# A graph network's first layer: another PSUM bank for the second pick of a step, a ranking's count taken half a step later, two buffers for a sorter's rows

## The chip, the cores and the metric

The kernel runs on one core of a Trainium2 chip. The metric is the device time of one execution in microseconds: the median of three runs of the kernel before is 4270.91 us (4266.38 to 4275.15).

## What is computed

Three layers of graph attention over 6250 nodes and 206250 edges (100000 pairs both ways, and a loop at each node), sorted by target node, with 64 features each. The reference, cut to what matters:

```python
for i in range(3):
    q = x @ Wq + bq; k = x @ Wk + bk; v = x @ Wv + bv; e = edge_attr @ We
    kj = k[src] + e
    alpha = sum(q[dst] * kj, -1) / sqrt(64)
    p = exp(alpha - segment_max(alpha, dst)[dst])
    w = p / segment_sum(p, dst)[dst]
    x = segment_sum((v[src] + e) * w[:, None], dst) + x @ Ws + bs
    x = relu(x)
    if i < 2: x = layer_norm(x, gamma[i], beta[i])
y = layernorm(x_in + log_softmax(x))
```

## The kernel before

Edges are cut into chunks of 512, and four chunks make a unit; a layer is a line of some 100 units. A unit is an online piece of attention: its edges' source features are gathered or picked, turned (transposed) so that PE can make scores from them, exponentiated, turned back and summed with weights into the nodes.

**The order** is written out by hand: the five engines take their instructions in the order of the code, with waits only where tiles are shared. The loop of layer 0 stands near the end of `main_path`; a step u of it works on several units at once:

- `weights` (the probabilities of unit u-2, turned by PE into bank `p`, copied by ACT);
- `turn(0)`, a piece of the sorter, `sums` (bank `g`, copied out by ACT at L1725), another piece of the sorter;
- `scores` of unit u-1 into bank `s` (L1673, L1678 on PE; DVE takes the row maximum, L1685 and L1687);
- `naturals` of unit u+1 and the **first pick** for unit u+2 (`picker.bank`, L1374 on PE into bank `g`, then ACT's copy into `kept`, L1383), then DVE's four hot masks for the next pick (`aim`, L1331);
- `turn(1)` (L1650 on PE, two copies on ACT at L1653), then `exps` of unit u-1 (L1692 on ACT: it reads bank `s`);
- the third piece of the sorter, then the **second pick** (L1374 and L1383 again, also in bank `g`), and the fourth piece.

Between these, gates on ACT (L635) release the gathers of POOL, and nodes are finished and projected (`finish`, `project`; both use bank `g` too, at L1532 and L1446).

**PSUM** has eight banks here: two each for the tags `a` and `x`, one each for `s`, `p`, `g` and `m`. Who writes a bank waits until the one who wrote it before has been read.

**A pick** takes source features out of node blocks with a matmul against 0/1 masks ("hot"), in place of gathering them: 24 matmuls of three bf16 parts, four blocks and two halves. In layer 0 two picks are due in each step.

**The sorter** runs in layer 0 alone, in four pieces a step (`move`). It puts a unit's edge features into the places that the picks ask for: `products` (L1064, bank `x`), `codes` (L1078, bank `m`), masks by DVE (`row`, L1053), then `drain`. `across` turns the placed features back into natural rows (PE, L1102, bank `m` or `a`), ACT copies them into a tile `eN` (L1104), and a DMA that ACT issues stores them (L1107). `index` (L1115 to L1120 on PE) makes indices and keys, which DVE and ACT copy out (L1123, L1129, L1134).

**A ranking** (L932 to L941) gives seats to edges by their kind, 23 rounds for each of four groups of chunks; the sorter takes a half round at two or three places of a step (`next(orders)`). The first half of a round is four matmuls with the masks `kinds` (L928), an activation on ACT that adds the count of the round before (`served`, L932), the next masks (L920) and the next count, taken by DVE from the last column (L935); the second half is two more DVE instructions (L939, L940). The tile `eN` is also used as room at a ranking's start and in the kernel's setup.

Of the kernel before, what the change touches and what calls it, by code (L numbers as in the profile page):

```python
# [9 lines left out]
F32 = mybir.dt.float32  # L10
# [9 lines left out]
P = 128  # L20
D = 64
L = 3
T = 4
# [419 lines left out]
def main_path(  # L443
# [89 lines left out]
    sorts = first_layer.enter_context(tc.tile_pool(name="sorts", bufs=2))  # L533

    def ps(tag):
        return psum.tile([P, 512], F32, tag=tag, name=f"ps_{tag}", bufs={"a": 2, "x": 2}.get(tag, 1))
# [356 lines left out]
    def ranking(i):  # L893

        those, n = ranks[i]
        seat = sorts.tile([P, CH], FP16, name="seat")[:n]
        half = sorts.tile([P, T, P], FP16, name="half", bufs=1)
        bins = sorts.tile([P, CH], FP16, name="bins", bufs=1)[:n]
        served = sorts.tile([P, WINDOWS + 2], F32, name="served", bufs=1)
        room = sorts.tile([P, 2 * T * D], F32, name="eN", bufs=1).bitcast(I32)  # L900
        runs = []
        for r, c0 in those:
            if runs and runs[-1][1] + runs[-1][2] == c0:
                runs[-1][2] += GC
            else:
                runs.append([r, c0, GC])
        for r, c0, m in runs:
            v = room[:, : m * T]
            nc.vector.tensor_scalar(v, src_b[:, c0 * T : (c0 + m) * T], P.bit_length(), None, ALU.logical_shift_right)
            nc.vector.tensor_copy(half[:, :, r : r + m], v.rearrange("p (c t) -> p t c", t=T))  # L910
        pc = ps("a")[:n]
        for t in range(T):
            nc.tensor.matmul(pc[:, t * P : (t + 1) * P], half[:, t, :n], same, start=True, stop=True)
        nc.scalar.copy(bins, pc)
        nc.vector.tensor_scalar(seat, bins, float(WINDOWS), 1000.0, ALU.is_gt, ALU.mult)
        nc.vector.memset(served[:, 0:1], -1.0)

        def kinds_of(h):
            kinds = sorts.tile([P, T, P], FP16, name="kinds", bufs=2)[:, :, :n]
            nc.vector.tensor_scalar(kinds, half[:, :, :n], float(h), None, ALU.is_equal)  # L920
            return kinds

        kinds = kinds_of(0)
        yield
        for h in range(WINDOWS + 1):
            pc = ps("a")[:n]
            for t in range(T):
                nc.tensor.matmul(  # L928
                    pc[:, t * P :], kinds[:, t], past[:, : CH - t * P], start=(t == 0), stop=(t == T - 1)
                )  # L930
            order = sorts.tile([P, CH], FP16, name="order", bufs=1)[:n]
            nc.scalar.activation(order, pc, AF.Identity, bias=served[:n, h : h + 1])  # L932
            if h < WINDOWS:
                kinds = kinds_of(h + 1)
            nc.vector.tensor_scalar(  # L935
                served[:n, h + 1 : h + 2], order[:, CH - 1 :], float(SL * min(h + 1, WINDOWS) - 1), None, ALU.min
            )
            yield
            nc.vector.scalar_tensor_tensor(order, bins, float(h), order, ALU.is_equal, ALU.mult)  # L939
            nc.vector.tensor_tensor(seat, seat, order, ALU.add)  # L940
            yield  # L941
        left = sorts.tile([P, CH], FP16, name="order", bufs=1)[:n]
        nc.vector.tensor_scalar(bins, bins, float(WINDOWS - 1), float(SL), ALU.min, ALU.mult)
        nc.vector.scalar_tensor_tensor(left, seat, -float(SL), bins, ALU.add, ALU.is_ge)
        nc.vector.tensor_tensor_scan(bins, left, left, float(SLOTS - 1), ALU.add, ALU.max)
        yield
        nc.vector.copy_predicated(seat, left.bitcast(mybir.dt.uint16), bins)
        spans = small.tile([P, WINDOWS + 1 + T], F32, name="spare")[:n]
        nc.vector.tensor_tensor(spans[:, : WINDOWS + 1], served[:n, 1:], least[:n], ALU.subtract)
        nc.vector.tensor_tensor(spans[:, WINDOWS + 1 :], most[:n], bins[:, P - 1 :: P], ALU.subtract)  # L950
        nc.vector.tensor_reduce(lacks[:n, i : i + 1], spans, AX.X, ALU.min)
        ranked[i] = seat
        yield
# [57 lines left out]
    class Move:  # L1011
# [86 lines left out]
        def across(self, i):  # L1098

            pn = ps("ma"[i])  # L1100
            for t in range(T):
                nc.tensor.transpose(pn[:, t * P : (t + 1) * P], self.eT[i][:, t * P : (t + 1) * P], ident)  # L1102
            eN = sorts.tile([P, 2 * T * D], F32, name="eN", bufs=1)
            nc.scalar.copy(  # L1104
                eN.rearrange("p (j t d) -> p t j d", j=2, d=D), pn.rearrange("p (t j d) -> p t j d", j=2, d=D)
            )
            nc.scalar.dma_start(eaP[self.k, :, 2 * i * T * D : 2 * (i + 1) * T * D], eN)  # L1107
# [35 lines left out]
    def sorter():  # L1143
# [11 lines left out]
        for i, _ in enumerate(first_ranks):  # L1155
            if i % 2:
                yield
        begun = 1
        orders = ranking(begun)
        for _ in mark(marked.pop(0)[0]):  # L1160
            pass
# [589 lines left out]
    release(0, 2 * LB)  # L1751
    locate(NK - 1, NC - (NK - 1) * P)
    first_ranks = ranking(0)
    active.append(begin(*groups[1]))
    active.append(late())
# [90 lines left out]
    for layer in range(L):  # L1846
# [5 lines left out]
        def drip(u, n=1):  # L1852
            points[0] += n
            lead = 2 * LB if not layer else min(2 * LB, LB + u)
            most = LB * (T - 1) if not layer else LB + 1
            release(layer, u * LB + min(points[0], most) * LB / most + lead, nc.scalar.copy)
            if not layer:
                next(first_ranks, None)

        if not layer:  # L1860
            picker = Picker(layer)
        for u in range(NU - 3):
# [52 lines left out]
            close_up(3) if close else step()  # L1915
            move(paces[2])
            while picker.due(u + 2):
                picker.bank(u + 2, "g")
            drip(u)
            picker.load()  # L1920
            move(paces[3])
# [14 lines left out]
        if more:  # L1936
            picker = Picker(layer + 1)
# [6 lines left out]
        u = NU - 3  # L1944
# [80 lines left out]
def kernel(tc: tile.TileContext, *args):  # L2025
    nc = tc.nc
    with tc.tile_pool(name="flag", bufs=1) as pool:
        irregular = pool.tile([1, 1], I32, name="irregular")
        with tc.manual_schedule(engines={ENG.PE, ENG.DVE, ENG.Activation, ENG.SP, ENG.Pool}):
            main_path(tc, *args, irregular)  # L2030
        flag = nc.values_load(irregular[0:1, 0:1], min_val=0, max_val=1, skip_runtime_bounds_check_because="a comparison")
        with tc.If(flag > 0):
            general_path(tc, *args)
# [34 lines left out]
```

## Time and profile before

| | |
|---|---|
| Median of three runs | 4270.91 us (4266.38 to 4275.15) |
| The profiled execution's own time | 4275.86 us |
| Its span, first to last instruction | 4274.1 us |
| Its mean granted clock of TensorE | 0.948 |
| L1374, picks into bank `x` (layers 1 and 2), PE | 836.7 us, 13248 matmuls |
| L1374, picks into bank `g` (layer 0), PE | 302.3 us, 4560 matmuls |
| L1692, exponentials, ACT | 204.2 us, 297 |
| L1104, natural rows' copies in layer 0, ACT | 57.3 and 56.7 us, 98 each |

How to read it: PE is TensorE's matmuls, PEld its weight loads, which overlap them; DVE, ACT, POOL and SP are the vector, scalar, GpSimd and sync engines. A group's row gives the line, engine, operation, tiles written and read, shapes and count, then its busy time in all, the mean of one in ns, and the idle time of the engine just ahead of its instructions with what ended most of it. In a row of waits stand the total, the times and the longest in us. In a timeline the first column is the start and the second the length in us; in brackets stand the idle time of the engine ahead of it and what ended that. A row of a stretch gives its bounds and length, busy time and count for PE, PEld, DVE, ACT and POOL, then the granted share of the clock, the DMA share and GB/s. Ends of matmuls are modelled.

### The profile page before, as it was taken

The page shows a single profiled execution, that of the slowest core. Times are in us where ns is not written, and L with a number is a line of the kernel's source. Part 1 is how long each engine was busy: PE and PEld are TensorE (multiplying, and loading weights), DVE is VectorE, ACT ScalarE, POOL GpSimd, SP SyncE. Part 2 cuts the span into 40 slices and gives each one's busy share as a digit, 9 for nine tenths or more (in the row PEclk, how much of TensorE's full clock was granted, in tenths as well). Part 3 has the DMA queues.
Part 4 walks back from the last instruction along what each step waited for, and adds up shares of the span by engine and source line. Part 5 has one row for each costly group of instructions (what it writes and reads, how often), then busy time and mean ns, then how long its engine had stood idle before and what let it go on. Part 6 is the DMA issues. An engine that isn't in the chain of part 4 may idle for free.

```text
span 4274.1 us, 125157 instructions
## 1 busy us (share of the span) xinstructions
PE 3681.7 (86%) x44542; PEld 2464.7 (58%) x44542; DVE 2891.1 (68%) x9241; ACT 2394.9 (56%) x7113; POOL 2067.3 (48%) x1910
## 2 busy tenths in 40 slices
PE   4679998889999999987889999998778998888885
PEld 2345555555555655654666666666456666666663
DVE  5566888787788777774566666666456666666664
ACT  2334555555555555543566666666536676666664
POOL 4454554555455665552444444444415444444442
PEclk9789999999999999997999999999879999999997
DMA  5447787787777888874677777777647777777773
GB/s 119 101 131 188 201 213 203 192 211 200 206 198 211 226 212 209 218 196 131 146 183 189 192 185 186 188 193 182 152 96 191 177 181 184 187 186 179 176 187 83
DMA packets 828647, 768.02 MB, mean 180 GB/s; under 512 B 393233, under 2 KB 628903, under 8 KB 828014
## 3 DMA queue, kind: packets, MB, share of 16 engines
q1 hardware_dynamic: 673282, 571.05, 54.2%
q10 hardware_dynamic: 93932, 126.48, 8.4%
q0 software_dynamic: 60800, 62.38, 7.8%
q8 instruction: 356, 5.83, 0.6%
q14 instruction: 277, 2.27, 0.2%
HBM read 599.30 MB, written 160.27 MB: 178 GB/s over the span
## 4 chain that ended last, share of the span: by engine, by line


## 5 line engine op out<-in xcount | busy, mean ns | idle before, releaser
L601 POOL DMA_INDIRECT feat<-in_x,gate x860 | 1050.6, 1222 | 884.4 <-ACT gate L635 686.4
L1331 DVE TENSOR_SCALAR hot<-key,rank 128x512 bf16<-128x512 f16 (+3 forms) x3024 | 908.2, 350 | 372.5 <-PE ps_x L1374 167.5
L601 POOL DMA_INDIRECT feat<-x,gate x816 | 796.8, 976 | 745.3 <-ACT gate L635 479.1
L1374 PEld LDWEIGHTS <-halves 128*64 128x64 bf16 x18144 | 963.4, 113 | 285.7 <-issue 206.1
L1374 PE MATMUL ps_x<-hot,halves 128*64 128x256 bf16 (+1 forms) x13248 | 836.7, 276 | 41.6 <-issue 31.2
L1717 PE MATMUL ps_g<-feat,probT 128*32 128x128 f32 x9672 | 436.5, 283 | 92.4 <-issue 61.6
L1064 PE MATMUL ps_x<-hit,rest 128*64 128x512 bf16 (+3 forms) x3200 | 459.1, 359 | 6.0 <-issue 5.1
L1409 ACT COPY featT<-kept 64x512 f32<-64x512 f32 x584 | 361.5, 619 | 144.3 <-PE ps_g L1374 42.6
L1053 DVE TENSOR_SCALAR hit<-ruler,pos 128x512 bf16<-128x512 f16 (+3 forms) x1600 | 422.9, 334 | 1.7 <-PE ps_m L1078 1.4
L1717 PEld LDWEIGHTS ps_g<-feat,probT 128*32 128x32 f32 x9672 | 286.5, 112 | 221.5 <-issue 175.6
L1685 DVE TENSOR_REDUCE most<-ps_s 128x1 f32<-128x512 f32 x297 | 204.1, 687 | 300.6 <-PE ps_s L1678 111.9
L601 POOL DMA_INDIRECT few<-x,gate x198 | 193.6, 978 | 379.4 <-ACT gate L635 113.0
L1374 PE MATMUL ps_g<-hot,halves 128*64 128x256 bf16 (+2 forms) x4560 | 302.3, 281 | 74.1 <-ACT kept L1383 28.5
L1653 ACT COPY featT<-ps_a 64x512 f32<-64x512 f32 x584 | 338.6, 580 | 15.6 <-PE ps_a L1650 4.1
L1678 PE MATMUL ps_s<-featT,q 128*32 128x512 f32 x2376 | 333.7, 621 | 2.9 <-ACT featT L1653 1.3
L1064 PE MATMUL ps_x<-hit,raw 128*64 128x512 bf16 (+3 forms) x1600 | 311.0, 367 | 4.5 <-issue 4.1
L1383 ACT COPY kept<-ps_x 128x256 f32<-128x256 f32 (+2 forms) x502 | 185.1, 370 | 210.8 <-remote 128.6
L635 ACT COPY gate<-src_b 128x1 int32<-128x1 int32 x1762 | 289.9, 191 | 8.7 <-ACT keys L1136 1.4
L1692 ACT ACTIVATE prob<-ps_s,part 128x512 f32<-128x512 f32 x297 | 204.2, 688 | 161.0 <-issue 48.7
L1704 PE MATMUL ps_p<-ident,prob 128*128 128x128 f32 (+1 forms) x1224 | 199.1, 286 | 91.9 <-ACT prob L1692 89.8
L1064 PEld LDWEIGHTS <-rest 128*64 128x64 bf16 x3200 | 203.8, 113 | 116.6 <-issue 30.0
L1725 ACT COPY part<-ps_g 128x128 f32<-128x128 f32 (+1 forms) x309 | 82.2, 266 | 273.0 <-PE ps_g L1717 43.8
(261 smaller groups left out, 5162.4 us busy)
## 6 DMA issues: line engine op xcount, KB each, us to landing
feat<-eaP SPq DMA_DIRECT2D x292, 512.0 KB
featT<-eaS SPq DMA_DIRECT2D x292, 512.0 KB
key<-keyS SPq DMA_DIRECT2D x712, 128.0 KB
raw<-in_ea SPq DMA_DIRECT2D x200, 256.0 KB
eaS<-eT ACTq DMA_DIRECT2D x200, 256.0 KB
eaP<-eN ACTq DMA_DIRECT2D x200, 256.0 KB
to<-toS SPq DMA_DIRECT2D x292, 128.0 KB
part<-part SPq DMA_DIRECT2D x600, 32.5 KB
```

Source lines behind the costliest of these rows:

```text
L601: nc.gpsimd.indirect_dma_start(out=spares[layer, k] if c is None else loaded[layer, k][:, c, t, 0], out_offset=None, in_=xts[layer][:, :], ...
L635: copy(gate, index[:, i : i + 1])
L1053: nc.vector.tensor_scalar(hit, ruler[:, : REACH[t]], self.pos[:, at : at + 1], None, ALU.is_equal)
L1064: nc.tensor.matmul(self.px[i][j * D : (j + 1) * D, : REACH[t]], self.part(i, part)[:, (j * T + t) * D : (j * T + t + 1) * D], self.hits[t, ...
L1331: nc.vector.tensor_scalar(hot[:, a:b].rearrange("p k w e -> p (k w e)"), self.keys[job][:, a * 2 * SL : b * 2 * SL], rank[:, h : h + 1], None,
L1374: nc.tensor.matmul(px[w * D : (w + 1) * D, a:b], third(halves[block >= EARLY][:, at : at + 1], part)[:, 0], made[h][:, a:b, w], start=(h = ...
L1409: nc.scalar.copy(featT[:D, :, w * P : (w + 1) * P], kept[0][w * D : (w + 1) * D, at : at + LB])
L1653: nc.scalar.copy(self.featT[:D, :, at : at + P], pt[h * D : (h + 1) * D])
L1678: nc.tensor.matmul(self.p_s[rows], self.q[:, j * STRIDE : j * STRIDE + W], self.featT[:, j, :], start=False, stop=True)
L1685: nc.vector.tensor_reduce(top[:n], self.p_s[:n], AX.X, ALU.max)
L1692: nc.scalar.activation(self.prob[:n], self.p_s[:n], AF.Exp, bias=self.part[:n, P : P + 1], accum_out=self.part[:n, P + 1 : P + 2],)
L1717: nc.tensor.matmul(p_g[rows, :].rearrange("n (h d) -> n h d", h=2), self.probT[:, t, rows], batch[:, c + j, t], start=(t == 0), stop=(t == ...
```

## The change

Three places of layer 0 change; nothing is computed otherwise.

```diff
@@ ranking @@
             if h < WINDOWS:
                 kinds = kinds_of(h + 1)
+            yield
             nc.vector.tensor_scalar(
                 served[:n, h + 1 : h + 2], order[:, CH - 1 :], float(SL * min(h + 1, WINDOWS) - 1), None, ALU.min
             )
-            yield
             nc.vector.scalar_tensor_tensor(order, bins, float(h), order, ALU.is_equal, ALU.mult)
@@ Move.across @@
-            eN = sorts.tile([P, 2 * T * D], F32, name="eN", bufs=1)
+            eN = sorts.tile([P, 2 * T * D], F32, name="natural", bufs=2)
@@ main_path, layer 0's step @@
             while picker.due(u + 2):
-                picker.bank(u + 2, "g")
+                picker.bank(u + 2, "s")
             drip(u)
```

The second pick writes bank `s` in place of bank `g`. The count of a round is taken at the head of the next half in place of the end of its own. The natural rows have a tile of their own in two buffers, and `eN` stays as the room of the rankings and the setup.

**PE, around the second pick of a step in the middle of layer 0** (the step whose timeline the prediction shows is of this form; `to` is the sorter's drained row of codes, `pickc` a constant). Before:

```order
L1118 MATMUL ps_a<-pickc,to 128x4
L1120 LDWEIGHTS to
L1120 MATMUL ps_a<-pickc,to 32x1
L1374 LDWEIGHTS halves [waits DVE_49]
L1374 MATMUL ps_g<-hot,halves 64x256 [waits Activation_49]
L1374 LDWEIGHTS halves
```

and with the change:

```order
L1118 MATMUL ps_a<-pickc,to 128x4
L1120 LDWEIGHTS to
L1120 MATMUL ps_a<-pickc,to 32x1
L1374 LDWEIGHTS halves [waits DVE_49]
L1374 MATMUL ps_s<-hot,halves 64x256 [waits Activation_49]
L1374 LDWEIGHTS halves
```

The instructions keep their places. The wait for ACT (`Activation_49` is its counter) is for another instruction: in the program before, its value is reached by the copy of the first pick (L1383), with the change by the exponential (L1692). All second picks of layer 0 have the new bank, and 95 of them wait so.

**ACT, the same place**, from the first pick's copy to the second's, with the change (before it is the same but for the names `eN` and `ps_g` and the waits of the natural rows' copies):

```order
L1383 COPY kept_253<-ps_g 128x16x16 [waits PE_49,Activation_49]
L1653 COPY featT<-ps_a 64x4x128 [waits PE_49]
L1653 COPY featT<-ps_a 64x4x128
L635 COPY gate<-src_b 128x1 [waits DMASW4_49]
L635 COPY gate<-src_b 128x1 [waits DMASW5_49]
L1692 ACTIVATE prob,part<-ps_s,part 128x512 [waits DVE_49]
L932 ACTIVATE order<-ps_a,served 112x512 [waits PE_49]
L1104 COPY natural<-ps_m 128x4x2x64 [waits DMAHW2_49,PE_49]
```

Between the first pick's copy and the exponential stand four instructions in both programs.

**DVE, at a ranking's round that falls between two picks of a step** (`src_b` and `keys` are what `index` makes). Before:

```order
L920 TENSOR_SCALAR kinds<-half 128x4x112
L935 TENSOR_SCALAR served<-order 112x1 [waits Activation_49]
L1123 TENSOR_SCALAR src_b<-ps_a 128x9 [waits PE_49]
L1129 CAST keys<-ps_a 4x2x4x16 [waits DMAHW4_49,DMAHW3_49]
L1129 CAST keys<-ps_a 4x2x4x16
L939 SCALAR_TENSOR_TENSOR order<-bins,order 112x512 [waits DVE_49]
```

and with the change:

```order
L920 TENSOR_SCALAR kinds<-half 128x4x112
L1123 TENSOR_SCALAR src_b<-ps_a 128x9 [waits PE_49]
L1129 CAST keys<-ps_a 4x2x4x16 [waits DMAHW4_49,DMAHW2_49]
L1129 CAST keys<-ps_a 4x2x4x16
L936 TENSOR_SCALAR served<-order 112x1 [waits Activation_49]
L939 SCALAR_TENSOR_TENSOR order<-bins,order 112x512 [waits DVE_49]
```

The count moves behind the indices and keys here, and behind the hits (L1053) where the half round falls into the sorter's second piece. DVE's other instructions stand as before.

## The prediction

> **What bounds the kernel now.** I read the page's first part, then a table of stretches, then the waits of layer 0 (the stage up to about 1965 us; all three edits lie in it), and last the timeline of single steps. The page has no chain of waits for this run (its part 4 is empty), so the bound is read from the busiest engine and its waits.
>
> ```profile
> PE 3681.7 (86%) x44542; PEld 2464.7 (58%) x44542; DVE 2891.1 (68%) x9241; ACT 2394.9 (56%) x7113; POOL 2067.3 (48%) x1910
> 400.00:1965.00 1565.00, 1416.07 (x16547) 903.52 (x16543) 1224.46 (x4143) 825.59 (x2422) 880.39 (x707) 0.97 0.78 206
> ```
>
> The second row is layer 0 past its start: length, busy time of PE, weight loads, DVE, ACT and POOL, then the granted clock. PE is busy for 1416.07 of 1565 us, DVE for 1224, ACT for 826. PE sets the pace, and what PE waits for is what can be won or lost: 148.9 us in some 88 steps, 1.7 us a step. The clock of 0.97 is also a number to keep: if it is either full or half, 3% missing means about 94 us at half speed.
>
> ```profile
> PE ps_g L1374 <- ACT kept L1383: 28.5, 32, 1.8
> ...
> PE ps_a L1115 <- ACT featT L1653: 21.8, 18, 3.9
> PE ps_g L1374 <- issue: 21.7, 36, 1.7
> ...
> PE ps_g L1374 <- DVE hot L1331: 11.4, 14, 1.9
> L1374 PE MATMUL ps_g<-hot,halves 128*64 128x256 bf16 (+3 forms) x4536 | 301.0, 282 | 72.0 <-ACT kept L1383 28.5 <-issue 21.7 <-DVE hot L1331 11.4
> ```
>
> These are the waits of 200 to 1965 us (total, times, longest) and the group of the picks' matmuls (its last number but the releasers is PE's idle time ahead of them). A pick is 24 matmuls, so 4536 are 189 picks, nearly two a step. 72.0 us of PE's idle time stand ahead of picks, most of it ahead of the second of a step, because that one writes the same bank as the first and waits until ACT has copied the first out (L1383). That wait is what the first edit takes away.
>
> **The first edit: the second pick writes the scores' bank.** Nothing is added or removed in instructions: 24 matmuls and one copy, as before. The wait changes. The scores of the step lie in that bank and are last read by the exponential on ACT (L1692), so the second pick must wait for it. One step, ACT and then PE:
>
> ```profile
> 1212.98 0.37 ACT L1383 COPY kept<-ps_g 128x256 f32<-128x256 f32 x1 [1.73 <-PE ps_m L1102]
> 1213.25 1.17 ACT L1653 COPY featT<-ps_a 64x512 f32<-64x512 f32 x2
> 1214.45 0.28 ACT L635 COPY gate<-src_b 128x1 int32<-128x1 int32 x2
> 1214.76 0.69 ACT L1692 ACTIVATE prob<-ps_s,part 128x512 f32<-128x512 f32 x1
> 1215.34 0.19 ACT L1692 ACTIVATION_READ_ACCUMULATOR prob<-ps_s,part 128x1 f32 x1
> ...
> 1213.15 0.19 PE L1120 MATMUL ps_a<-pickc,to 128*32 128x1 bf16 x4
> 1213.40 1.50 PE L1374 MATMUL ps_g<-hot,halves 128*64 128x256 bf16 x24
> ```
>
> Here the second pick starts at 1213.40, just as the first pick's copy ends. ACT takes its instructions in order, and behind that copy stand two feature copies (1.17), two gates (0.28) and the exponential (0.69), which ends at 1215.45. So the new wait ends **2.05 us later than the old one**, and it can never end earlier, because the exponential stands behind the copy in ACT's order. Queued behind the second pick on PE are the ranking's matmuls, the sorter's products and the next step's transposes; none can pass it.
>
> There is a second kind of step, where PE has already waited for the feature copies:
>
> ```profile
> 1269.95 0.31 PE L1115 MATMUL ps_a<-to,keyc 128*4 128x352 bf16 x1 [0.89 <-ACT featT L1653]
> ...
> 1270.44 1.50 PE L1374 MATMUL ps_g<-hot,halves 128*64 128x256 bf16 x24
> ...
> 1270.23 0.69 ACT L1692 ACTIVATE prob<-ps_s,part 128x512 f32<-128x512 f32 x1
> ```
>
> There the exponential ends at 1270.92, 0.48 us after the pick's start. And where ACT must load its function table first (1.28 us more), it is later still:
>
> ```profile
> 1800.12 1.50 PE L1374 MATMUL ps_g<-hot,halves 128*64 128x256 bf16 x24 [1.39 <-ACT kept L1383]
> ...
> 1801.47 1.28 ACT L1692 ACT_TABLE_LOAD   x1
> 1802.76 0.69 ACT L1692 ACTIVATE prob<-ps_s,part 128x512 f32<-128x512 f32 x1
> ```
>
> That is 3.33 us. Going through all 94 steps in the timeline, from this one to this one,
>
> ```profile
> 422.34 1.50 PE L1374 MATMUL ps_g<-hot,halves 128*64 128x256 bf16 x24 [0.49 <-ACT kept L1383]
> 423.70 0.69 ACT L1692 ACTIVATE prob<-ps_s,part 128x512 f32<-128x512 f32 x1
> ...
> 1900.82 0.95 PE L1374 MATMUL ps_g<-hot,halves 128*64 128x128 bf16 x24 [0.36 <-ACT kept L1383]
> 1902.17 0.69 ACT L1692 ACTIVATE prob<-ps_s,part 128x512 f32<-128x512 f32 x1
> ```
>
> (a few more lie ahead of and behind these two), the exponential's end less the pick's start is 1.9 to 2.1 us in 36 steps (73.3 us together), above 2.4 in 15 (45.6), 0.8 to 1.9 in 10 (15.2), 0.1 to 0.65 in 19 (8.4), and in 14 the exponential is done first. **Sum: 142.5 us.** The row that reads the accumulator ends some 0.1 us after the exponential, which adds about 8 us in 80 steps if the release comes with it; in some steps the pick would have waited for its hot masks anyway, which takes about 8 us off. I take +142.
>
> Bounds. PE can make the time good only out of later waits that are not PE's own doing. All of PE's idle time of layer 0, less the 72.0 us ahead of picks, is about 80 us, and 21.8 of it (L1115) stand ahead of the second pick. If all of the rest, some 60, swallowed the delay, +80 would be left; nothing lets more than 150 come of it directly.
>
> **What a PE that waits longer does to its clock.**
>
> ```profile
> 1204.10 1.08 PE L1717 MATMUL ps_g<-feat,probT 128*32 128x128 f32 x32
> ...
> 1222.61 1.94 PE L1717 MATMUL ps_g<-feat,probT 128*32 128x128 f32 x32 [1.92 <-DVE rows_now L1535]
> 1222.40:1225.40 3.00, 2.79 (x42) 2.08 (x44) 2.80 (x18) 1.23 (x7) 0.00 (x0) 0.50 0.02 5
> ...
> 440.36 2.63 PE L1374 MATMUL ps_g<-hot,halves 128*64 128x256 bf16 x24 [1.72 <-ACT gate L635]
> 440.60:444.00 3.40, 3.40 (x28) 2.29 (x24) 2.14 (x8) 1.55 (x7) 2.05 (x2) 0.51 0.86 219
> ...
> 1947.25 0.62 PE L1078 MATMUL ps_m<-hit,stamp 128*32 128x512 bf16 x4 [1.94 <-ACT eN L1104]
> 1946.00:1952.00 6.00, 4.75 (x32) 2.05 (x33) 5.72 (x18) 3.08 (x12) 6.00 (x1) 0.50 0.24 90
> ```
>
> After 1.92 us of idle time the granted clock is 0.50 for about 3.4 us, and the same 32 matmuls take 1.94 instead of 1.08. Past 400 us, PE has 20 such gaps of 1.5 us or more in layer 0 (the rows show the first, one in the middle and the last but one, each with the clock of the stretch behind it), and 17 of them come with a stretch at half speed. With the new wait added to the old one, about 63 second picks would follow a gap of 1.5 us or more, where about 10 do now: some 50 more, at 17 in 20 about 43 more stretches, each up to 1.7 us of lost work (half of 3.4). That is between 0 and 73 us; I take 60, since the row shows nearly the full loss. The clock of layer 0 would fall from 0.97 to about 0.92.
>
> The Trainium skill, page "TensorE: Matmul & The Clock Gate", section "Why this matters for your kernels", advises no PE gaps above about 3 us between bursts. By that rule gaps of 2 to 3 us cost no clock; the row above, at 1.92 us, differs, so I go by the row and keep the rule as a rival.
>
> **The second edit: the ranking's count half a step later.**
>
> ```profile
> DVE served L935 <- ACT order L932: 73.9, 32, 5.2
> ...
> ACT eN L1104 <- DMA eaP<-eN: 36.4, 24, 4.3
> ...
> DVE served L935 <- ACT gate L635: 24.4, 9, 4.5
> ...
> DVE served L935 <- issue: 18.0, 11, 2.8
> ```
>
> DVE stands still for 116 us in front of the count (L935), waiting for ACT's activation of the same half step. Moved, it stands where that activation is long done, and the hits, hot masks or key copies behind it come earlier, by 5.2 us at the longest of these waits and some 2 us at most of them. The next activation reads the count a further half step on, so no wait moves there. Same instructions. DVE is busy for 1224 of 1565 us and not the bound; what PE gets is bounded by its waits for DVE:
>
> ```profile
> PE ps_g L1446 <- ACT kept L1383: 7.0, 6, 2.5
> ...
> PE ps_g L1717 <- issue: 4.8, 11, 1.0
> PE ps_g L1717 <- DVE rows_now L1535: 4.6, 3, 1.9
> ...
> PE ps_g L1717 <- ACT probT L1707: 3.1, 4, 1.1
> ```
>
> The 11.4 us for hot masks ahead of picks are now covered by the wait for the exponential. The rest is the sums' wait (L1717), 12.5 us, of which I count 8.
>
> **The third edit: two buffers for natural rows.** It removes ACT's 36.4 us of waiting for the store of the rows before. ACT is idle for nearly half of layer 0; the copy waits for nothing else and is not read by PE, so I count 10 of the 36 as reaching PE (through the weights' copy and the next first pick's copy). Bounds 0 and 36. The first edit also frees the counts' bank for the projection: L1446's 7.0 us go. Gains together 25 us, bounds 0 and about 60.
>
> **Sum.** 142 + 60 - 25 = +177 us on the profiled execution's own 4275.9 (span 4274.1 and 1.8 around it): 4453. The median of the runs, 4270.9, is 5 below the profiled execution, so I forecast **4448 us** (+4.1%).
>
> **The rivals.**
> - *The wait is carried, the clock holds* (the skill's rule; as a mechanism: the half speed follows something else that happens with the gaps). 142 - 25 = +117: 4388. For it: 3 of 20 gaps were followed by none. Against: 17 of 20.
> - *Absorbed*: PE's later waits of a step swallow what they can and the clock hardly changes. 142 - 60 - 25, some +57: 4328. Against it: apart from the picks PE waits under 1 us a step, mostly "issue".
> - *Worse*: a slower PE also makes ACT later at the next exponential, and nothing of the gains arrives: 150 + 73 + 30 = +253, 4524.
> - *Faster*: ACT's two stalls set when the exponential ends. If ACT stood still for its stores and DVE's keys in the steps that matter, the exponential would come some 2 us earlier without them, the second pick would wait for neither, and of the 72.0 us ahead of picks and the 19.5 at L1717 and L1446 some 80 would go: 4271 - 80 = 4191. It decides only if the exponential gains over 2.05 us on the first pick's copy; but between those two nothing waits (the rows at 1213 follow each other within 0.06 us), so I see no room for it.
>
> **How the numbers follow.** Forecast 0.60 (4448, own range 4410 to 4490), clock holds 0.16, absorbed 0.10, worse 0.06, faster 0.05, nothing to be measured 0.03. The range leaves out the faster end and about half of the absorbed and the worse: 4335 to 4520. Chances: faster by over 0.2% (about what a measurement of this kernel can tell from no change) 0.05, within 0.2% 0.03, slower 0.92.
>
> **What would show it.** In the profile after: PE's waits at L1374 on the scores' bank, ended by ACT's L1692, some 200 us in all of layer 0 where picks now have 72; layer 0 longer by 150 to 200 us and layers 1 and 2 as before; the clock of layer 0 near 0.92; the waits of DVE at the count and of ACT for the natural rows' store almost gone. I am wrong if the exponential's wait is there but layer 0 isn't longer (absorbed), if the clock stays at 0.97, or if the second picks start no later after the first pick's copy than now.

## The result and the profile after

| | before | after |
|---|---|---|
| Median (runs) | 4270.77 us (4) | 4395.61 us (4), 4385.78 to 4419.28 |
| The profiled execution, its span | 4275.86 us, 4274.1 us | 4386.75 us, 4384.9 us |
| Its mean granted clock | 0.948 | 0.932 |

The changed kernel is slower: ratio 1.0284, 95% interval 1.0254 to 1.0314. The forecast was 4448 us, 52 us too much; the time lies in its range. The medians differ by 124.8 us, the two profiled executions by 110.8 us of span; the account below is of the latter. From here on, layer 0 ends at one fixed point of the program, the 99th of the scores' rows, at 1973 us before and 2084 us after.

The profile's page after, its first lines (busy time of each engine):

```profile
span 4384.9 us, 125148 instructions
...
PE 3697.6 (84%) x44542; PEld 2496.3 (57%) x44542; DVE 2903.7 (66%) x9241; ACT 2400.9 (55%) x7113; POOL 2104.6 (48%) x1910
```

The stretches of before, layer 0 past its start and then the rest, with that end of layer 0 (columns as in the table of the profile before):

```profile
400.00:1973.00 1573.00, 1420.41 (x16588) 905.21 (x16584) 1225.67 (x4149) 827.03 (x2425) 880.39 (x707) 0.97 0.78 206
1973.00:4274.00 2301.00, 1980.37 (x25723) 1391.59 (x25723) 1425.45 (x4294) 1438.19 (x4304) 999.88 (x1024) 0.94 0.70 171
```

The same two of after:

```profile
400.00:2084.00 1684.00, 1432.83 (x16569) 934.05 (x16565) 1234.52 (x4142) 831.86 (x2423) 907.26 (x706) 0.94 0.73 192
2084.00:4384.00 2300.00, 1985.27 (x25723) 1395.55 (x25723) 1426.95 (x4297) 1438.36 (x4304) 1002.58 (x1024) 0.94 0.70 171
```

The whole difference lies in layer 0: 1573 became 1684 us (+111), and the rest took 2301 and 2300. In layer 0 PE is busy 12.4 us longer (1420.41 to 1432.83), so nearly all of it is idle time: 152.6 us (1573.00 less 1420.41) became 251.2. The clock of the stretch fell from 0.97 to 0.94.

Where PE waits, in layer 0 after: the two groups of the picks' matmuls (busy, mean of one, then the idle time ahead of them), from the table of groups:

```profile
L1374 PE MATMUL ps_s<-hot,halves 128*64 128x256 bf16 (+3 forms) x2295 | 184.8, 322 | 205.9 <-ACT prob L1692 150.6 <-DVE hit L1053 37.6 <-issue 17.1
L1374 PE MATMUL ps_g<-hot,halves 128*64 128x256 bf16 (+3 forms) x2256 | 140.7, 271 | 3.1 <-issue 3.0
```

The second picks (`ps_s`) have 205.9 us of idle time ahead of them, the first picks (`ps_g`) 3.1, together 209.0 where all picks had 72.0: +137. These rows count from 200 us; the idle time in all grew by 98.6 us from 400 us on and by 98.5 from 200 us on. All other idle time of PE fell by 38 (98.6 less 137), so the account of layer 0 is **137 - 38 + 12 = 111 us**.

One step in the timeline after:

```profile
1034.70 1.50 PE L1374 MATMUL ps_g<-hot,halves 128*64 128x256 bf16 x24
...
1037.54 0.19 PE L1120 MATMUL ps_a<-pickc,to 128*32 128x1 bf16 x4
1037.57 0.37 ACT L1383 COPY kept<-ps_g 128x256 f32<-128x256 f32 x1 [1.93 <-PE ps_m L1102]
1037.84 1.17 ACT L1653 COPY featT<-ps_a 64x512 f32<-64x512 f32 x2
1039.04 0.28 ACT L635 COPY gate<-src_b 128x1 int32<-128x1 int32 x2
1039.35 0.69 ACT L1692 ACTIVATE prob<-ps_s,part 128x512 f32<-128x512 f32 x1
1039.93 0.19 ACT L1692 ACTIVATION_READ_ACCUMULATOR prob<-ps_s,part 128x1 f32 x1
1040.03 0.58 ACT L1104 COPY natural<-ps_m 128x512 f32<-128x512 f32 x1
1040.18 1.50 PE L1374 MATMUL ps_s<-hot,halves 128*64 128x256 bf16 x24 [2.45 <-ACT prob L1692]
```

PE has done what it can by 1037.73, ACT's copy of the first pick, which released the second pick before, starts at 1037.57 and ends at 1037.94, and the second pick starts at 1040.18, 0.14 us behind the exponential's end (1039.35 + 0.69). Of the 95 second picks of layer 0 in this trace, 88 start 0.14 us behind an exponential's end, whatever releaser the view names; so the 37.6 us put down to hits (L1053) and 10 of the 17.1 of "issue" are the same wait, 198 us of the 205.9 in all.

DVE's waits at the count, after (one line further down now):

```profile
DVE served L936 <- issue: 6.9, 15, 0.5
DVE served L936 <- ACT order L932: 2.3, 2, 1.8
```

They were 116 us at L935: the count's edit did what it was made for. ACT's 36.4 us for the store of the natural rows are gone altogether, but most of that need not be the second buffer's doing. The same copies also wait for PE's transposes, before and then after:

```profile
ACT eN L1104 <- PE ps_a L1102: 68.5, 43, 6.3
...
ACT natural L1104 <- PE ps_a L1102: 82.3, 73, 6.4
```

The prediction said that the copy "waits for nothing else", which these 68.5 us contradict; part of what the store gave up went to this wait. And in the kernel with the bank alone (first experiment below), which has one buffer as before, the wait for the store is down to 3.5 us:

```profile
ACT eN L1104 <- DMA eaP<-eN: 3.5, 3, 2.1
```

In that kernel's second run, on another chip, it is 20.2 us, where the count alone, with both picks in bank `g`, has 106.8. So with the second pick in bank `s` the second buffer has little left to take away. The bank's edit costs more than the other two bring.

### The profile page after: what moved, and what is told of

It is laid out like the page before. It is cut to its first block, busy times and chain, and to the rows that moved or that the text cites. A ratio compares the mean times of both kernels' runs of the same rounds, so it can differ in the third digit from the quotient of the medians.

```text
span 4384.9 us, 125148 instructions
## 1 busy us (share of the span) xinstructions
PE 3697.6 (84%) x44542; PEld 2496.3 (57%) x44542; DVE 2903.7 (66%) x9241; ACT 2400.9 (55%) x7113; POOL 2104.6 (48%) x1910
## 4 chain that ended last, share of the span: by engine, by line
## 5 line engine op out<-in xcount | busy, mean ns | idle before, releaser
L601 POOL DMA_INDIRECT feat<-in_x,gate x860 | 1085.2, 1262 | 956.8 <-ACT gate L635 761.8
L1374 PEld LDWEIGHTS <-halves 128*64 128x64 bf16 x18144 | 992.7, 115 | 418.9 <-issue 345.2
L1409 ACT COPY featT<-kept 64x512 f32<-64x512 f32 x584 | 361.2, 619 | 140.7 <-PE ps_s L1678 34.3
L1053 DVE TENSOR_SCALAR hit<-ruler,pos 128x512 bf16<-128x512 f16 (+3 forms) x1600 | 415.4, 328 | 22.3 <-PE ps_m L1078 12.4
L1374 PE MATMUL ps_s<-hot,halves 128*64 128x256 bf16 (+2 forms) x2640 | 208.9, 318 | 234.2 <-ACT prob L1692 151.5
L1653 ACT COPY featT<-ps_a 64x512 f32<-64x512 f32 x584 | 338.4, 580 | 8.4 <-PE ps_a L1650 4.1
L1383 ACT COPY kept<-ps_x 128x256 f32<-128x256 f32 (+2 forms) x502 | 185.4, 370 | 225.1 <-remote 129.1
L1692 ACT ACTIVATE prob<-ps_s,part 128x512 f32<-128x512 f32 x297 | 204.1, 687 | 161.6 <-PE ps_a L1404 50.8
L1064 PEld LDWEIGHTS <-rest 128*64 128x64 bf16 x3200 | 207.9, 116 | 119.2 <-issue 34.1
L1704 PE MATMUL ps_p<-ident,prob 128*128 128x128 f32 (+1 forms) x1224 | 200.8, 288 | 88.7 <-ACT prob L1692 87.3
L1704 PEld LDWEIGHTS ps_p<-ident,prob 128*128 128x128 f32 (+1 forms) x1224 | 139.2, 145 | 144.9 <-ACT prob L1692 108.6
```

What stands on the lines that cost most here:

```text
L601: nc.gpsimd.indirect_dma_start(out=spares[layer, k] if c is None else loaded[layer, k][:, c, t, 0], out_offset=None, in_=xts[layer][:, :], ...
L1053: nc.vector.tensor_scalar(hit, ruler[:, : REACH[t]], self.pos[:, at : at + 1], None, ALU.is_equal)
L1064: nc.tensor.matmul(self.px[i][j * D : (j + 1) * D, : REACH[t]], self.part(i, part)[:, (j * T + t) * D : (j * T + t + 1) * D], self.hits[t, ...
L1374: nc.tensor.matmul(px[w * D : (w + 1) * D, a:b], third(halves[block >= EARLY][:, at : at + 1], part)[:, 0], made[h][:, a:b, w], start=(h = ...
L1409: nc.scalar.copy(featT[:D, :, w * P : (w + 1) * P], kept[0][w * D : (w + 1) * D, at : at + LB])
L1653: nc.scalar.copy(self.featT[:D, :, at : at + P], pt[h * D : (h + 1) * D])
```

## The experiments

They stand in three groups, each on one chip with its own runs of the kernel before, whose median was 4321.05 us (9 runs) for the first group, 3817.75 (12) for the second and 3809.51 (7) for the third. That spread is a finding of its own (last section); here only ratios to the kernel before on the same chip are compared, or kernels of one group. The expectations are in us of the first measurement, and the kernel before took other times in each group, so they are read as ratios to its 4270.77. The counts of PE's idle time below are from 200 us to the end of layer 0, if no other start is given.

| kernel | group | median us | ratio to before, 95% |
|---|---|---|---|
| bank alone | 1 | 4464.46 | 1.0348 (1.0322 to 1.0374) |
| count and natural rows | 1 | 4305.66 | 0.9964 (0.995 to 0.9978) |
| whole change, exponential earlier | 1 | 4382.76 | 1.0157 (1.0132 to 1.0183) |
| before, exponential earlier | 1 | 4383.53 | 1.014 (1.012 to 1.016) |
| count alone | 2 | 3782.61 | 0.9909 (0.989 to 0.9928) |
| natural rows alone | 2 | 3799.81 | 0.9947 (0.993 to 0.9964) |
| second pick in bank `p`, with the other edits | 2 | 3803.66 | 0.9968 (0.9953 to 0.9983) |
| whole change, unread matmuls in the wait | 2 | 3918.3 | 1.0259 (1.0236 to 1.0282) |
| whole change | 3 | 3894.07 | 1.0211 (1.0162 to 1.0259) |
| whole change, unread matmuls in the wait | 3 | 3920.5 | 1.0298 (1.0242 to 1.0354) |
| bank alone | 3 | 3901.24 | 1.0221 (1.0167 to 1.0275) |
| count alone | 3 | 3775.04 | 0.9897 (0.9849 to 0.9945) |

### The bank alone, and the two other edits alone

The bank alone, against the kernel before:

```
-                picker.bank(u + 2, "g")
+                picker.bank(u + 2, "s")
```

> The bank alone (second pick into the scores' bank; count and natural rows as before). If the loss is the wait for the exponential, PE's idle time ahead of second picks is near 205 us as with the whole change and the time is 4390 to 4425 us: at or somewhat above the whole change (4395), since the two other edits give a little back. If the moved count or the extra buffer made part of the loss, the time is 4330 to 4370.

Measured: 1.0348, a larger loss than that of the whole change, and inside the first expectation (1.028 to 1.036 as a ratio). The idle time ahead of its second picks is 200.6 us, near the 205 that was expected:

```profile
L1374 PE MATMUL ps_s<-hot,halves 128*64 128x256 bf16 (+3 forms) x2280 | 199.2, 341 | 200.6 <-ACT prob L1692 174.7 <-DVE hit L1053 17.2 <-issue 5.5
```

The other two edits together, second pick in its old bank:

```
+            yield            (ahead of the count)
...
-            yield            (behind it)
...
-            eN = sorts.tile([P, 2 * T * D], F32, name="eN", bufs=1)
+            eN = sorts.tile([P, 2 * T * D], F32, name="natural", bufs=2)
```

> The count and the natural rows alone (second pick in bank g as before). If the wait for the exponential is the whole loss: 4245 to 4270 us, DVE's 116 us at the count and ACT's 36 us at the natural rows nearly gone, PE's idle time in layer 0 lower by 0 to 25 us. If these two edits cost something: 4285 or more.

Measured: 0.9964, a small gain, as expected if the wait for the exponential is the whole loss (0.994 to 1.000). Layer 0 past 400 us of the two, the bank alone first:

```profile
400.00:2143.00 1743.00, 1473.29 (x16582) 956.95 (x16582) 1228.76 (x4145) 833.20 (x2425) 858.48 (x707) 0.92 0.70 186
```

and the two other edits:

```profile
400.00:1988.00 1588.00, 1419.03 (x16533) 896.94 (x16532) 1222.11 (x4136) 823.05 (x2419) 940.98 (x704) 0.97 0.77 203
```

So the loss belongs to the bank. Between these two kernels layer 0 differs by 155 us, of which 54.3 are longer busy time of PE (1473.29 less 1419.03) at a clock of 0.92 against 0.97, and 101 idle time. In this variant the cost of the clock that the prediction had feared is there.

### Is it the exponential? Moving it ahead

If the second pick's wait for the exponential is the loss, the loss must go when the exponential comes earlier. In both kernels here the step's exponentials are issued ahead of `turn(1)`, the transposes of features whose two copies ACT takes, instead of behind it. The edit:

```
-            this.turn(1, lambda: drip(u))
...              (the exponentials)
+            this.turn(1, lambda: drip(u))
```

The whole change with it:

> The whole change, but the exponential is put ahead of turn(1), so on ACT it stands right behind the first pick's copy, ahead of the two feature copies and the gates. If the loss is the exponential's place in ACT's order, the second pick starts some 0.8 us after the first pick's copy in place of 2.1, its idle time falls from 208 us to about 120, and the time to 4300 to 4350 (the feature copies come 0.7 us later, which L1115 feels in the steps where PE waits for them). If it is the bank itself (writes beside reads of the scores' bank), idle time and time stay: 4380 to 4410.

The kernel before with it, as a control:

> The control of the run before it: the kernel before with the exponential ahead of turn(1), all else as before. It shows what the exponential's move alone costs: the feature copies come 0.7 us later, felt at L1115 in the 18 steps or more in which PE waits for them: 4270 to 4295 us. Below 4265 would say that an early exponential helps by itself.

Measured: 1.0157 and 1.014. As a ratio the first lies where the exponential's place was expected to put it (1.007 to 1.019) and not where the bank itself would (1.026 to 1.033). With the exponential early, the change costs nothing (4382.76 against 4383.53 us); with the exponential in its place it cost 2.84% in the first measurement, and the bank alone 3.48% on this chip. The second picks' row of the whole change with the early exponential:

```profile
L1374 PE MATMUL ps_s<-hot,halves 128*64 128x256 bf16 (+3 forms) x2280 | 169.3, 303 | 110.9 <-ACT prob L1692 75.7 <-DVE hit L1053 19.6 <-issue 7.7
```

Their idle time is 110.9 us, about the 120 expected. So it is the exponential's place that the change loses by. That it "costs nothing" is a net figure: PE's idle time ahead of all picks is still 53 us longer than in the control (115.0 against 62.3; the bank alone has 134 more than the kernel with the two other edits), and its other idle time is 58 us shorter (138.0 against 196.1). The control was expected near the kernel before (1.000 to 1.006) and is a miss: the move itself costs 1.4%. Some of PE's waits of layer 0 in it:

```profile
PE ps_a L1115 <- ACT featT L1653: 44.1, 20, 6.0
...
PE ps_g L1717 <- ACT probT L1707: 22.8, 16, 3.9
...
PE ps_g L1446 <- ACT kept L1383: 14.6, 6, 7.5
```

These were 21.8, 7.0 and 7.0 in the profile before, in the first measurement. The feature copies (L1653) now stand behind the exponential in ACT's order, and PE waits for them twice as long. The copy of the transposed probabilities (L1707) and the pick's copy (L1383) have kept their places; why PE waits longer for them is not shown. In the whole change with the early exponential the second picks still wait for it, half as long (75.7 us against 150.6), and PE for the feature copies:

```profile
PE ps_s L1374 <- ACT prob L1692: 75.7, 48, 4.2
PE ps_a L1115 <- ACT featT L1653: 35.4, 14, 6.7
```

### The count alone and the natural rows alone

The count alone:

> The moved count alone. DVE's wait at the count falls from 116 us to under 20. If DVE's standing still reached PE (through the hot masks and the finished nodes): 4245 to 4262 us. If DVE's gain is idle time of an engine that isn't the bound: 4265 to 4275.

The natural rows alone:

> The two buffers of natural rows alone. ACT's 36 us of waiting for the store go. If they reached PE through the weights' copy and the next first pick's copy: 4250 to 4265 us. If not: 4266 to 4275.

Measured: 0.9909 and 0.9947. PE's waits for hot masks ahead of picks in layer 0, natural rows alone:

```profile
PE ps_g L1374 <- DVE hot L1331: 34.1, 20, 3.8
```

and count alone:

```profile
PE ps_g L1374 <- DVE hot L1331: 11.7, 12, 1.9
```

The count gains more than either expectation (0.994 to 0.998 at best), the natural rows about the best that was expected (0.995). Of the two kernels, the one with the moved count waits 22 us less for hot masks (34.1 to 11.7), and its layer 0 is 34 us shorter in the profile (1806 to 1772 us). That speaks for the count's gain arriving at the picks: DVE no longer stands still at the count, and the hot masks come earlier. It is not a clean comparison. The two kernels differ by both edits, the profiled executions lie further apart (38.8 us) than the medians (17.2), and there is no trace of the kernel before on this chip. That the natural rows' edit alone gains 0.5% is shown by the time only.

### Another bank for the second pick

Since the scores' bank is bad for its last reader, bank `p` was tried in its place, with the other two edits:

```
-                picker.bank(u + 2, "s")
+                picker.bank(u + 2, "p")
```

> Count and natural rows as in the change, second pick into bank p. There it waits for DVE's copy of the naturals (which in the step at 1213 us ended 0.4 us ahead of the first pick's copy), and the next step's turned probabilities (L1704) wait for the second pick's copy. If only the place of the last reader decides, the second pick's idle time is at or below the 63 us of before and the time 4235 to 4270. If L1704's new wait takes it back: 4275 or more, with idle time at L1704.

Measured: 0.9968, in the range of the first expectation (0.992 to 1.000), better than the kernel before, worse than the count alone. Its own control, the two other edits with bank `g`, was run in the first group only (0.9964), so what bank `p` by itself gains or costs is not separated. PE's waits of layer 0:

```profile
PE ps_p L1704 <- ACT kept L1383: 29.8, 24, 2.8
PE ps_p L1374 <- DVE hot L1331: 16.0, 18, 2.3
```

The picks hardly wait now (16.4 us in all, under the 63 that was expected at most), but the probabilities' transposes (L1704), which use that bank next, wait 29.8 us for the pick's copy: the second expectation's wait is there too.

### Does the half speed behind the gaps cost time?

Five matmuls of 128x512 ahead of each second pick of layer 0, into the bank it has left; nothing reads them, and they lie in the wait for the exponential. The edit, on the changed kernel:

```
+                if u >= U0:
+                    spin = ps("g")
+                    for _ in range(5):
+                        nc.tensor.matmul(spin, codeT, this.to, start=True, stop=True)
                 picker.bank(u + 2, "s")
```

> The whole change with five more matmuls (128x512, bf16, some 1.1 us) ahead of each second pick, into bank g; they are read by nobody. They fill part of the gap, so the clock should not fall: layer 0 near 0.97 in place of 0.93. If the half-speed stretches were a good part of the loss, the time falls to 4340 to 4375 in spite of the added work; if they cost little, it stays or rises: 4390 to 4440 (in the steps of the second kind the five have no gap to fill, some 0.6 us in 35 steps).

Measured: 1.0259, between the two expectations (up to 1.024, from 1.028), with no run of the whole change in that group to hold it against. So it was repeated beside the whole change, the bank alone and the count alone:

> The whole change once more, so that it stands on one chip beside its parts. If the ratio belongs to the program: 1.026 to 1.031, as in the first measurement (1.0284). If this chip is one on which PE's waits are short (the kernel before near 3820 us instead of 4270), the theory that the loss is the exponential's 2 us in each step still gives about +110 us, 1.029; the theory that a lower clock adds to it gives less there, 1.015 to 1.022.

> The whole change with five matmuls of 128x512 (about 1.1 us) ahead of each second pick of layer 0, into the bank that the pick has left; nothing reads them. They lie in the wait for the exponential, so that PE has no gap of more than some 1.2 us there. If the half speed behind the gaps costs time (the prediction's +60 us), the second picks' own matmuls take less than in the whole change and the time is 20 to 60 us below it. If the half speed costs nothing that sets the end, it is the same or up to 30 us longer (steps whose wait is shorter than 1.1 us).

> The scores' bank for the second pick alone, without the later count and the two buffers. If the other two edits help the whole change by what they help the kernel before (0.3 to 0.5%), this is 1.003 to 1.006 times the whole change. If they help more when the exponential is what is waited for, because they also bring ACT's queue forward, it is 1.006 to 1.012 times the whole change.

> The ranking's count half a step later, alone, second pick in its old bank. Measured once at 0.991 of the kernel before. If that holds whichever chip it runs on: 0.988 to 0.993, the fastest kernel of this study. If it held only where PE's other waits are short: 0.994 to 0.999, no better than the two edits together (0.9964).

Measured: 1.0211, 1.0298, 1.0221 and 0.9897. The whole change did not repeat its first ratio (1.026 to 1.031 expected), and the +110 us of the exponential's wait are not there either: the medians differ by 85. By the letter that is the range expected if a lower clock adds to the wait. The traces say otherwise: the wait itself is shorter on this chip, 139.4 us ahead of second picks against 205.9. Layer 0 of the whole change on this chip, its second picks and its stretch:

```profile
L1374 PE MATMUL ps_s<-hot,halves 128*64 128x256 bf16 (+3 forms) x2280 | 153.0, 287 | 139.4 <-ACT prob L1692 126.4 <-DVE hot L1331 6.3 <-DVE hit L1053 2.9
...
400.00:1884.00 1484.00, 1327.34 (x16081) 868.92 (x16079) 1190.06 (x4011) 809.22 (x2348) 912.24 (x684) 0.97 0.78 211
```

the same two of the count alone:

```profile
L1374 PE MATMUL ps_g<-hot,halves 128*64 128x256 bf16 (+3 forms) x4512 | 280.8, 275 | 30.5 <-ACT kept L1383 12.6 <-DVE hot L1331 12.1 <-DVE sk L1447 3.7
...
400.00:1772.00 1372.00, 1309.37 (x16042) 837.99 (x16038) 1184.40 (x4007) 798.49 (x2347) 917.11 (x685) 0.99 0.85 228
```

and the second picks with the unread matmuls ahead of them:

```profile
L1374 PE MATMUL ps_s<-hot,halves 128*64 128x256 bf16 (+2 forms) x2256 | 148.4, 283 | 31.1 <-ACT prob L1692 27.7 <-DVE hit L1053 1.3 <-DVE hot L1331 0.8
```

Against the count alone, the whole change's layer 0 is 112 us longer (1484 against 1372): 109 us more idle time ahead of picks (139.4 less 30.5), 16 of busy time, 13 less of other idle time. The account has the shape of the one above; the direct wait is nearly all of it.

With the unread matmuls the idle time in front of second picks falls to 31.1 us, and the picks' own matmuls gain 4.6 us (153.0 to 148.4); the kernel is not faster but 26 us slower by the medians (3920.5 against 3894.07), as expected if the half speed costs nothing that sets the end. The test says less than that. Layer 0 of the two profiled executions is about the same length (1880 and 1884 us); the later layers, which the edit does not touch, were some 15 us longer, and why stays open. Within layer 0 the half-speed time past 400 us fell only from 78.5 to 58.0 us, which by the clock alone is worth 10 us at most. In 21 of 90 steps the unread matmuls themselves held up the second pick (it starts 0.71 us behind the exponential in place of 0.14), which costs about 12 us. So on this chip the half speed that the test took away cost some 10 us at most, beside the 109 of the direct wait. It was not tried on a chip like the first group's, where it would matter more.

Bank alone against whole change: 3901.24 against 3894.07, 7 us, with runs that overlap (3885.62 to 3904.07 against 3890.4 to 3895.66): 1.0018 times the whole change, below both expectations. The count alone gains 34 us here (3809.51 to 3775.04); with the second pick behind the exponential, count and natural rows together bring 7 us or nothing. The likely reason that the gains do not add up is that they lie at the same place: the count shortens the picks' wait for hot masks, and the bank puts a longer wait of its own over it. In the bank alone on this chip, without the count's edit, that wait is short already:

```profile
PE ps_s L1374 <- DVE hot L1331: 7.5, 6, 2.1
```

On the slower chips it may be otherwise: there the bank alone (1.0348) lies above the whole change (1.0284), by more than the 0.4% that the other two edits gain by themselves, but the two stand in different measurements.

The fastest kernel of the study is the count alone, 0.9909 and 0.9897 in two groups (0.988 to 0.993 was expected of the second), faster than both the kernel before and the change. On a chip like the first group's it was not run by itself; with the natural rows it gave 0.9964 there.

## Why the prediction was right, and where its size was off

- **The bound and the new wait: right.** The second pick waits for the exponential instead of for the first pick's copy. Forecast +142 us; the idle time ahead of picks grew by 137 in the profile, and 88 of 95 second picks start 0.14 us behind the exponential. The extra 8 us for the accumulator's row were right too: it ends at 1040.12 in the step shown, and the pick starts at 1040.18. That the loss hangs on the exponential's place is shown by the pair with the exponential ahead, where the picks' idle time grows by 53 us in place of 134.
- **"What a PE that waits longer does to its clock", +60 us: the term that was mis-sized.** Of the 66 us between the sum (177) and the account (111), 48 are this term, 13 the gains and 5 the wait. PE's busy time in layer 0 grew by 12.4 us. The count of gaps was about right: 76 gaps of 1.5 us or more past 400 us after, 20 before, so 56 more (forecast 50). But 46 of the 76 had a stretch of half speed behind them, against 17 of 20 before: 29 more, not 43. By length: 33 of 44 gaps above 2.5 us, 9 of 23 between 2 and 2.5, 4 of 9 between 1.5 and 2. And a stretch cost less than the one row on which I had built: half-speed time in that part of layer 0 rose by 103 us (92.0 to 194.6), and PE was busy for 170.5 us of it in place of 84.4. At half the work that would be 43 us of longer busy time, and 12.4 are seen. The step at 1232.72 shows one that does cost:

```profile
1231.61 0.31 PE L1115 MATMUL ps_a<-to,keyc 128*4 128x352 bf16 x1 [2.28 <-ACT featT L1653]
...
1232.72 2.65 PE L1374 MATMUL ps_s<-hot,halves 128*64 128x256 bf16 x24 [0.55 <-ACT prob L1692]
```

  After 2.28 us and 0.55 us of waiting the 24 matmuls take 2.65 us where they took 1.50 at 1034.70. Over all second picks the group's mean is 322 ns against 271 for the first picks; for the picks together that is 24.5 us more busy time (184.8 + 140.7 against 301.0), and PE's other instructions were busy some 12 us less, which takes half of it back; why they were is not shown. The bank alone, in its group, had about the forecast cost (54.3 us more busy time, with 276.5 us at half speed against 88.7). It differs from the whole change by the two other edits and stands in another measurement, and no run tells which of them makes the term larger, so its size is not settled.
- **The clock as a rival.** "The wait is carried, the clock holds" forecast 4388 us. The time came out 8 us from there and below the forecast's own range (4410 to 4490), but not by that mechanism alone: the clock of layer 0 did fall, from 0.97 to 0.94 (I had said 0.92). The traces bear out neither rule for the clock as a sharp one. Gaps above 3 us were followed by half speed in 18 of 19 cases in the profile after and in 23 of 23 in the bank alone. Gaps between 1.5 and 2.5 us were so in 13 of 32 cases after, 10 of 13 before and 19 of 26 in the bank alone; on the third group's chip 1 of the 52 between 1.0 and 1.5 was. The Trainium skill, page "TensorE: Matmul & The Clock Gate", section "Why this matters for your kernels", advises no PE gaps above about 3 us between bursts. These runs agree with it above 3 us. Below, half speed follows too often to call such gaps safe, and after the change it follows less often than my 17 in 20 (46 of 76 gaps of 1.5 us or more, 61 of 75 in the bank alone).
- **The gains, -25 us: nearly the right number, for another reason.** The idle time of PE elsewhere fell by 38. It is mostly not the two edits: in the first group the bank alone, which lacks them, has 39 us less of it than the kernel that has only them (93.1 against 131.7), and on the third group's chip the two edits beside the bank bring 7 us or nothing. So it is delay that PE's later waits took up, which I had put at nothing in the sum and only in the rival "absorbed", there with 60. That my number came near is luck. The reason I gave for the hot masks, that their wait is "covered by the wait for the exponential", is what the third group bears out.
- **Layers 1 and 2 as before: right** (2301 and 2300 us). The waits at the count and for the natural rows' store went as forecast, but the bank alone takes away most of the second one.

## What to carry to other kernels

A tile that moves to another PSUM bank takes over the wait for that bank's last reader: look up where this reader stands in its engine's order, not how free the bank looks. Add up the distance step by step in the timeline; here it gave 142 us against 137 measured, while a clock penalty scaled up from one row was five times too large (in the bank alone it was about right). Test edits apart: one that shortens a wait (the count, 1% by itself) is worth little beside one that puts a longer wait over the same place.

## What the runs showed of the hardware that was not expected

**The same program took 4271, 4321, 3818 and 3810 us in four measurements**, the last three on three chips (the first one's is not on record), each steady over its runs (4313 to 4329 and 3811 to 3827, for instance). The granted clock differs little (0.945 and 0.957 in the first and the second group), and the exponential takes 0.69 us in both. One thing that differs is how late ACT's copy of the first pick comes. In the profile after, in the step shown above, that pick ends at 1036.20 and the copy starts at 1037.57, 1.37 us later. The same place on the third group's chip, whole change:

```profile
944.94 1.50 PE L1374 MATMUL ps_g<-hot,halves 128*64 128x256 bf16 x24
...
946.54 0.37 ACT L1383 COPY kept<-ps_g 128x256 f32<-128x256 f32 x1 [0.56 <-PE ps_g L1374]
...
947.77 0.19 PE L1120 MATMUL ps_a<-pickc,to 128*32 128x1 bf16 x4
...
948.57 0.69 ACT L1692 ACTIVATE prob<-ps_s,part 128x512 f32<-128x512 f32 x1
...
949.40 1.50 PE L1374 MATMUL ps_s<-hot,halves 128*64 128x256 bf16 x24 [1.44 <-ACT prob L1692]
```

There it starts 0.10 us behind the pick (946.44 to 946.54), and the second pick waits 1.44 instead of 2.45 us. The median over the steps of layer 0 is 1.51 us and 0.10 us; the kernel before in the first measurement and the bank alone in the first group have 1.76 and 1.74. Ends of matmuls are modelled, so these rows cannot tell whether PE was really slower there or its signal later.

The trace's records of PE's counter, on which ACT waits, speak for the signal (some of these records are missing). In the step above, ten matmuls that count it up start between 1034.95 and 1037.55, the pick's own four 0.33 us apart. The counter's steps come at 1036.57 and then nine times between 1037.34 and 1037.77, at most 0.08 us apart, and the copy starts at 1037.57 among them. On the third group's chip the steps of the pick come at 945.48, 945.81, 946.14 and 946.46, as far apart as its matmuls. Over layer 0 past 400 us, 47% of the counter's steps lie under 0.09 us behind the one before in the profiles before and after, and 26% in the whole change on the third group's chip, where the modelled ends of the same matmuls have 23 to 24% in all three. Not every signal is late: DVE's row maximum starts 0.07 us behind the scores' modelled end on both, and the second pick 0.14 us behind the exponential's. Why the counter's steps come late and close together in one measurement and not in the other stays open.

The loss is smaller on the faster chip: the bank alone gave 1.0221 (1.0167 to 1.0275) there and 1.0348 (1.0322 to 1.0374) in the first group; for the whole change, 1.0211 (1.0162 to 1.0259) and 1.0284 (1.0254 to 1.0314), the intervals just touch.
